# Mamba dt projection: contraction over 16 rows, or over 128 rows with zeros

## Chip, cores, metric

The kernel runs on one core of a Trainium2 chip. The metric is the device time in microseconds of one execution, median of the runs shown.

## What is computed

The program is a stack of layers on an input of shape (2, 256, 56, 56): local attention with convolution, a position term, a six-layer Mamba block with a norm, a gated feed-forward, a causal attention and a mixture of eight experts. Only the Mamba block is touched. Per layer, with 512 inner channels, 16 states and a dt rank of 16:

```python
xz = x @ in_w
u, z = jnp.split(xz, 2, axis=-1)
uc = silu(depthwise_conv4(u) + cb)
x_dbl = uc @ xp_w                      # 48 columns: 16 dt, 16 B, 16 C
dt_r, Bm, Cm = x_dbl[..., :16], x_dbl[..., 16:32], x_dbl[..., 32:]
dt = softplus(dt_r @ dt_w + dt_b)      # the dt projection: contraction over 16
A = -exp(A_log)
h = exp(dt * A) * h + (dt * u) * B     # scan over time, per channel and state
y = sum over states of h * C, plus u * D
out = (y * silu(z)) @ out_w
```

All of it is in float32.

## The kernel before

Three phases follow each other: `conv_phase`, `mamba_phase`, `tail_phase`. They share nothing but tensors in DRAM. In `mamba_phase` the 3136 tokens of an image are cut into 7 chunks of 448 (`T`). The list `chunks` (L788) runs over 2 images, 6 layers and 7 chunks: 84 chunks. Channels lie on the partitions, in 4 blocks (`NB`) of 128.

A chunk has two parts that run one chunk apart. The scan of chunk j takes 32 steps (`order`, L784): each makes its decays on ACT (`decays`, L806), its inputs dt·u·B on POOL (`inputs`, L823, after a small copy of the state by ACT, L822), a scan on DVE (`scan`, L844), the product with C on DVE or, for the 14 steps in `on_pool`, on POOL (L836), a copy of the state on ACT (`keep`, L832). Every second step, `gather` sums over the states on TensorE into the PSUM tile `acc` (L857: four 32-column matmuls beside each other for each pair of tiles); every eighth step it begins with the skip matmul (L852, weights `w_sk`), and `gate` on DVE (L867) multiplies the sum with z. A tile `x` is written by POOL, scanned, multiplied and read by the gather, and only then free again: the pool `mb_x` holds 9.

Between the steps of chunk j lies the preparation of chunk j + 1, each in small pieces: projections of u and z (`project`, L560), convolution by four matmuls with diagonal weights (`u_convolve`, L578), the projection on 48 columns (`x_project`, L610), then the pieces around the change:

- `x_keep` (L618): ACT copies the 48 rows from PSUM into the SBUF tile `xd`; a DMA stores its rows 16 to 47 (B and C) to DRAM (L620), and four more bring them back into `bc`, repeated over partitions (L623).
- `dt_project` (L631), once for each block of 128 channels, in the order 0, 2, 3, 1: one matmul with weights `w_dt` (16 rows by 128 columns) and the first 16 rows of `xd` as moving operand (448 columns).
- `dt_keep` (L637): ACT adds the bias and moves the result from PSUM to SBUF.
- `dt_softplus` (L642) on ACT, `dt_out` (L648 to L652): dt goes to DRAM, POOL forms dt·u (L650), and that goes to DRAM too; `repeat` (L780) brings both back.

All these projections share one PSUM tile, `mm` (pool `mb_pmm`, one buffer), so the next projection waits until ACT has moved the last one out. The order of the instructions on every engine is written by hand: the table `places` gives each piece a place in units of scan steps, `steps` does so for the steps, and all events are sorted by place (L999) and issued in that order. `dt_project` of blocks 0, 2 and 3 lie at 19.3, 20.0 and 20.3, that of block 1 at 22.8; a skip matmul and a gather lie between them.

Weights are loaded once per layer and image by `load_layer` (L510), all DMAs on the queue of SP: `vec`, `w_in`, `w_xp`, `w_dt`, `w_out`, in that order. `w_dt` has one buffer in the pool `mb_weights`, `xd` one in `mb_one`. In the profile a float32 matmul of the program shows as two records (672 records for 336 dt projections).

Of the kernel before, what the change touches and what calls it, by code (L numbers as in the profile page):

```python
# [10 lines left out]
F32 = mybir.dt.float32  # L11
# [7 lines left out]
P = 128  # L19
# [14 lines left out]
DI = 512  # L34
NB = DI // P
DS = 16
DTR = 16
# [15 lines left out]
def chunk(c, n=NT):  # L53
    return slice(c * n, (c + 1) * n)
# [399 lines left out]
def mamba_phase(ctx: ExitStack, tc: tile.TileContext, I, t1_d, t2_d):  # L454
# [8 lines left out]
    nc = tc.nc  # L463
    ctx.enter_context(tc.manual_schedule())
    T, R = MT, MT + 3
    cp = ctx.enter_context(tc.tile_pool(name="mb_const", bufs=1))
    wtp = ctx.enter_context(tc.tile_pool(name="mb_weights", bufs=1))
    one = ctx.enter_context(tc.tile_pool(name="mb_one", bufs=1))
# [36 lines left out]
    def mm():  # L505
        if early[0]:
            return pda.tile([P, 1024], F32, name="da")[:, :512]
        return pmm.tile([P, 512], F32, name="mm", tag="mm")

    def load_layer(layer):  # L510

        vec = wtp.tile([P, V_L], F32, name="vec", bufs=2)
        nc.sync.dma_start(vec, I["mamba_vec"][layer])
        w_in = wtp.tile([P, 2, 2 * DI], F32, name="w_in")
        nc.sync.dma_start(w_in, I["in_w"][layer].rearrange("(k p) o -> p k o", p=P))
        w_xp = wtp.tile([P, NB, DTR + 2 * DS], F32, name="w_xp")
        nc.sync.dma_start(w_xp, I["xp_w"][layer].rearrange("(k p) o -> p k o", p=P))
        w_dt = wtp.tile([DTR, DI], F32, name="w_dt")
        nc.sync.dma_start(w_dt, I["dt_w"][layer])
        w_out = wtp.tile([P, NB, C], F32, name="w_out", bufs=2)  # L520
        nc.sync.dma_start(w_out, I["out_w"][layer].rearrange("(k p) o -> p k o", p=P))
        am = wtp.tile([P, NB * DS], F32, name="am", bufs=2)
        state = wtp.tile([P, NB, 4, 4], F32, name="state", bufs=2)
        tail = wtp.tile([P, NB, 3], F32, name="tail", bufs=2)
        w_sk = wtp.tile([P, NB, P], F32, name="w_sk", bufs=2)
        w_cv = wtp.tile([P, NB * 4, P], F32, name="w_cv")
        L = dict(
            nw=vec[:, 0:2], cb=vec[:, 18:22], dtb=vec[:, 22:26], w_sk=w_sk, w_in=w_in,
            w_xp=w_xp, w_dt=w_dt, w_out=w_out, w_cv=w_cv, am=am, state=state, tail=tail,
        )  # L530
        yield L

        nc.scalar.activation(am, vec[:, 26:90], AF.Exp)
        nc.gpsimd.tensor_scalar(am, am, TINY, -1.0, ALU.max, ALU.mult)
        nc.gpsimd.memset(state, 0.0)
        nc.gpsimd.memset(tail, 0.0)

        for n in range(NB * 4):
            nc.scalar.activation(w_cv[:, n, :], ident, AF.Copy, scale=vec[:, 2 + n : 3 + n])
            if n % 2:  # L540
                yield
        for n in range(NB):
            nc.scalar.activation(w_sk[:, n, :], ident, AF.Copy, scale=vec[:, 90 + n : 91 + n])
            if n % 2:
                yield
# [2 lines left out]

    M = {"dt": cp.tile([P, NB, T + 4], F32, name="dt")[:, :, 3 : T + 3]}
    us = [cp.tile([P, T + 3], F32, name=f"u{n}") for n in range(2)]
    hzs = [cp.tile([P, 2 * NB, T], F32, name=f"hz{n}") for n in range(2)]
# [2 lines left out]
    def project(j, at):  # L556
        Q = QS[j + 1]
        ps = M["mm"] = mm()[:, :T]
        for k in range(2):
# [8 lines left out]
    def u_keep(j, d):  # L568
        tail = layer_of(j + 1)["tail"][:, d, :]
        u = M["u", d] = us[d % 2]  # L570
        nc.scalar.copy(u[:, 0:3], tail)
        nc.scalar.copy(u[:, 3:], M["mm"])
        nc.scalar.copy(tail, u[:, T:])

    def u_convolve(j, d):
        ps = M["mm"] = mm()[:, :T]
        for k in range(4):
            nc.tensor.matmul(  # L578
                ps, lhsT=layer_of(j + 1)["w_cv"][:, 4 * d + k, :], rhs=M["u", d][:, k : k + T],
                start=(k == 0), stop=(k == 3),  # L580
            )

    def hz(j):

        Q = QS[j + 1]
        Q["hz"] = hzs[(j + 1) % 2]
        return Q["hz"]

    def u_add(j, d):
        nc.scalar.activation(  # L590
            hz(j)[:, d, :], M["mm"], AF.Identity, bias=layer_of(j + 1)["cb"][:, d : d + 1]
        )
# [21 lines left out]

    def x_keep(j):

        xd = M["xd"] = one.tile([DTR + 2 * DS, T], F32, name="xd")
        nc.scalar.copy(xd, M["mm"])  # L618
        bc_d = dp.tile([2 * DS, T], F32, name="bc_d")
        nc.sync.dma_start(bc_d, xd[DTR:, :])  # L620
        bc = QS[j + 1]["bc"] = bcs[(j + 1) % 2]
        for n in range(4):
            nc.sync.dma_start(  # L623
                bc[chunk(n, HD), :, :T],
                bc_d.rearrange("(m n) t -> n m t", n=4)[n].unsqueeze(0).to_broadcast([HD, 8, T]),
            )
        QS[j + 1]["dt_d"], QS[j + 1]["dtu_d"] = {}, {}

    def dt_project(j, d):
        ps = M["mm"] = mm()[:, :T]  # L630
        nc.tensor.matmul(  # L631
            ps, lhsT=layer_of(j + 1)["w_dt"][:, chunk(d, P)], rhs=M["xd"][:DTR, :],
            start=True, stop=True,
        )

# [155 lines left out]
    def layer_of(j):  # L791
        return layers[chunks[j][:2]]
# [87 lines left out]
    def load(j):  # L880

        QS[j + 2] = {}
        b, layer, c = chunks[j + 2]
        if (b, layer) not in layers:
            loading[j] = load_layer(layer)
            layers[b, layer] = next(loading[j])
# [5 lines left out]
    def load_rest(j):  # L892
# [12 lines left out]
        (u_project, 3): 12.31697, (u_keep, 3): 12.96717, (u_convolve, 3): 14.04980,  # L905
        (u_add, 3): 14.56347, (z_project, 1): 15.43302, (z_keep, 1): 16.33985, (u_silu,): 17.02689,
        (x_project,): 18.08430, (x_keep,): 18.92340, (dt_project, 0): 19.34668,
        (dt_keep, 0): 19.40825, (dt_project, 2): 20.04090, (dt_keep, 2): 20.17101,
        (dt_project, 3): 20.28119, (dt_keep, 3): 20.60584, (dt_project, 1): 22.80017,
        (dt_keep, 1): 23.31716, (dt_softplus,): 23.33757, (dt_out, 0): 24.14324,  # L910
        (z_project, 2): 24.29994, (z_keep, 2): 24.73754, (z_project, 3): 24.99253,
# [74 lines left out]
    for j in range(nj):  # L986
        b, layer, c = chunks[j]
# [550 lines left out]
```

## Time and profile before

| | us |
|---|---|
| median of 3 runs | 9790.64 (9786.32 to 9806.52) |
| profiled execution, its own time | 9795.2 |
| its span, first to last instruction | 9793.4 |
| Mamba part, from about 614 us to about 8490 us | 7880 |

| engine | busy us | share of the span |
|---|---|---|
| PE (TensorE) | 8175.8 | 83% |
| DVE (VectorE) | 8083.2 | 83% |
| POOL (GpSimd) | 7545.9 | 77% |
| ACT (ScalarE) | 6611.1 | 68% |

In the profile a group of instructions is a line of the kernel, an engine, an operation and its tiles, then the count, the total busy time, the mean of one in ns, and the idle time of the engine ahead of it with what ended it. PEclk is the share of TensorE's clock that its throttle granted, 0.873 over the span. The last part, after 8490 us, is another phase and is bound by TensorE at full clock.

### The profile page before, as it was taken

To read this page: it belongs to the slowest core of one execution; us is meant where nothing else is said; L and a number is where in the kernel's file an instruction comes from. 1 tells how busy PE (TensorE), PEld (TensorE's weight loads), DVE (VectorE), ACT (ScalarE), POOL (GpSimd) and SP (SyncE) were. 2 spreads that over 40 slices of the span, in tenths; PEclk is the share of its full clock that TensorE was granted. 3 is DMA by queue.
4 is the path that set the end of the run, shared out by engine and by line. 5 is a ranking of instruction groups with operands and counts; after the bars stand their busy time and mean duration, and the time that the engine had idled before them with its cause. 6 is when DMAs were issued, how large, how long until landed. Compare 5 with 4: busy or idle time off the path is not lost. (4 is left out here: it accounts for less than half of the span.)

```text
span 9793.4 us, 102137 instructions
## 1 busy us (share of the span) xinstructions
PE 8175.8 (83%) x31362; PEld 3469.1 (35%) x31362; DVE 8083.2 (83%) x6388; ACT 6611.1 (68%) x15130; POOL 7545.9 (77%) x5146
## 2 busy tenths in 40 slices
PE   9878888888888887888888878888888888699999
PEld 6543333332222222333322223222222233255555
DVE  3339999999999999998999999999999999685453
ACT  1127777777777777777777777777777777534443
POOL 1339999899999999999999999999999999511110
PEclk9988888888888888888888888888888888799999
DMA  2235555555555555555555555555555555301111
GB/s 81 68 97 121 119 133 124 135 124 118 132 121 121 130 122 125 127 133 134 131 118 128 126 129 122 124 131 118 132 121 121 133 121 123 107 19 36 42 39 38
DMA packets 681949, 1083.42 MB, mean 111 GB/s; under 512 B 83532, under 2 KB 673169, under 8 KB 681169
## 3 DMA queue, kind: packets, MB, share of 16 engines
q1 hardware_dynamic: 681398, 1076.90, 47.7%
q8 instruction: 246, 4.03, 0.2%
q14 instruction: 305, 2.50, 0.1%
HBM read 891.71 MB, written 184.91 MB: 110 GB/s over the span
## 5 line engine op out<-in xcount | busy, mean ns | idle before, releaser
L823 POOL TENSOR_TENSOR x<-dtur,bc 128x900 f32<-128x900 f32 x2688 | 4712.4, 1781 | 285.4 <-PE acc L857 272.0
L806 ACT ACTIVATE da<-dtr,am 128x451 f32<-128x451 f32 x5376 | 3400.6, 638 | 367.0 <-DVE x L844 220.5
L844 DVE TENSOR_TENSOR_SCAN da<-da,x 128x902 f32<-128x902 f32 x1512 | 3050.7, 2030 | 358.5 <-POOL x L823 176.5
L844 DVE TENSOR_TENSOR_SCAN x<-da,x 128x902 f32<-128x902 f32 x1176 | 2353.9, 2022 | 51.8 <-ACT da L806 34.7
L836 POOL TENSOR_TENSOR x<-x,bc 128x896 f32<-128x896 f32 x1176 | 2074.0, 1773 | 63.0 <-DVE x L844 59.1
L560 PE MATMUL mm<-xn,w_in 128*128 128x448 f32 x2652 | 1344.7, 635 | 494.8 <-ACT hz L590 244.9
L836 DVE TENSOR_TENSOR x<-da,bc 128x896 f32<-128x896 f32 x1512 | 1610.3, 1083 | 83.8 <-ACT state L832 49.4
L857 PE MATMUL acc<-x,sum_w 128*32 128x448 f32 x10752 | 1498.2, 633 | 21.2 <-POOL x L836 18.9
L578 PE MATMUL mm<-u,w_cv 128*128 128x448 f32 x2656 | 1186.0, 593 | 203.3 <-ACT res L715 184.5
L560 PEld LDWEIGHTS mm<-xn,w_in 128*128 128x128 f32 x2652 | 504.3, 211 | 1382.5 <-issue 459.0
L578 PEld LDWEIGHTS mm<-u,w_cv 128*128 128x128 f32 x2656 | 515.8, 204 | 866.4 <-issue 426.2
L631 PE MATMUL mm<-xd,w_dt 16*128 16x448 f32 x664 | 482.8, 817 | 232.8 <-ACT dt L637 134.6
L822 ACT COPY x<-state 128x2 f32<-128x2 f32 x2688 | 466.4, 189 | 287.2 <-PE acc L857 280.5
L857 PEld LDWEIGHTS acc<-x,sum_w 128*32 128x32 f32 x10752 | 268.3, 118 | 1043.4 <-issue 511.7
L708 PE MATMUL mm<-hz,w_out 128*128 128x448 f32 x1344 | 550.4, 552 | 79.6 <-ACT res L715 65.2
L852 PE MATMUL acc<-hz,w_sk 128*128 128x448 f32 x672 | 469.4, 791 | 41.9 <-DVE hz L867 41.8
L832 ACT COPY state<-da 128x2 f32<-128x2 f32 x1512 | 229.5, 157 | 390.0 <-DVE x L836 323.8
L1386 DVE TENSOR_TENSOR hid<-hid,cb 128x784 f32<-128x784 f32 x128 | 140.7, 1101 | 423.3 <-ACT hid L1383 394.5
L610 PE MATMUL mm<-hz,w_xp 128*48 128x448 f32 x664 | 339.6, 666 | 140.0 <-ACT state L832 140.0
L650 POOL TENSOR_TENSOR dtu<-dt,hz 128x448 f32<-128x448 f32 x336 | 325.3, 979 | 125.9 <-ACT state L832 110.6
L590 ACT ACTIVATE hz<-mm,vec 128x448 f32<-128x448 f32 x332 | 207.0, 624 | 277.8 <-PE mm L578 277.8
L708 PEld LDWEIGHTS mm<-hz,w_out 128*128 128x128 f32 x1344 | 241.8, 190 | 395.5 <-issue 189.6
(222 smaller groups left out, 9167.3 us busy)
## 6 DMA issues: line engine op xcount, KB each, us to landing
dtr<-dt_d SPq DMA_DIRECT2D x1344, 224.0 KB
dtur<-dtu_d SPq DMA_DIRECT2D x1344, 224.0 KB
bc<-bc_d SPq DMA_DIRECT2D x336, 448.0 KB
dt_d<-dt SPq DMA_DIRECT2D x336, 224.0 KB
dtu_d<-dtu SPq DMA_DIRECT2D x336, 224.0 KB
cb<-comb_d SPq DMA_DIRECT2D x128, 196.0 KB
t<-t_d SPq DMA_DIRECT2D x28, 448.0 KB
w_in<-in_in_w SPq DMA_DIRECT2D x12, 1024.0 KB
```

The lines of the kernel that those rows point to most:

```text
L560: nc.tensor.matmul(ps, lhsT=layer_of(j + 1)["w_in"][:, k, chunk(at, P)], rhs=Q["xn"][:, k, :], start=(k == 0), stop=(k == 1),)
L578: nc.tensor.matmul(ps, lhsT=layer_of(j + 1)["w_cv"][:, 4 * d + k, :], rhs=M["u", d][:, k : k + T], start=(k == 0), stop=(k == 3),)
L610: nc.tensor.matmul(ps, lhsT=layer_of(j + 1)["w_xp"][:, d, :], rhs=hz(j)[:, d, :], start=(d == 0), stop=(d == NB - 1),)
L631: nc.tensor.matmul(ps, lhsT=layer_of(j + 1)["w_dt"][:, chunk(d, P)], rhs=M["xd"][:DTR, :], start=True, stop=True,)
L708: nc.tensor.matmul(ps, lhsT=layer_of(j - 1)["w_out"][:, d, chunk(k, P)], rhs=QS[j - 1]["hz"][:, d, :], start=(d == 0), stop=False,)
L806: nc.scalar.activation(D[i][:, chunk(g, R)], dtr[:, 2 * pr + g, :], AF.Exp, scale=L["am"][:, col : col + 1],)
L822: nc.scalar.copy(x[:, :, 0:1], states(i))
L823: nc.gpsimd.tensor_tensor(x[:, :, 1:], Q[k][1][:, 2 * pr : 2 * pr + 2, :], wide(Q["bc"][:, ng, :]), ALU.mult)
L836: engine.tensor_tensor(both(X[i])[:, :, 1 : T + 1], both(h)[:, :, 1 : T + 1], wide(QS[j]["bc"][:, 4 + ng, :T]), ALU.mult,)
L844: nc.vector.tensor_tensor_scan(h, D[i], X[i], 0.0, ALU.mult, ALU.add)
L852: nc.tensor.matmul(acc[0][:, :T], lhsT=L["w_sk"][:, k, :], rhs=Q["hz"][:, k, :], start=True, stop=False,)
L857: nc.tensor.matmul(acc[0][chunk(g, HD), :T], lhsT=sum_w, rhs=both(X[i - 1 + g // 2])[:, g % 2, 1 : T + 1], start=False, stop=(ng == 3), ti ...
```

## The change

`xd` and `w_dt` become tiles of 128 rows that are allocated once, in the pool of constants, and set to zero once, by two memsets on POOL at the start of the phase. The copy from PSUM and the load of the weights fill the same rows as before; rows 16 to 127 of `w_dt` stay zero, and so do rows 48 to 127 of `xd`. Rows 16 to 47 of `xd` hold B and C, which the zero rows of `w_dt` multiply. The dt projection contracts over all 128 rows.

```diff
-        w_dt = wtp.tile([DTR, DI], F32, name="w_dt")
-        nc.sync.dma_start(w_dt, I["dt_w"][layer])
+        nc.sync.dma_start(w_dt[:DTR, :], I["dt_w"][layer])
...
-            w_xp=w_xp, w_dt=w_dt, w_out=w_out, w_cv=w_cv, am=am, state=state, tail=tail,
+            w_xp=w_xp, w_out=w_out, w_cv=w_cv, am=am, state=state, tail=tail,
...
+    xd = cp.tile([P, T], F32, name="xd")
+    nc.gpsimd.memset(xd, 0.0)
+    w_dt = cp.tile([P, DI], F32, name="w_dt")
+    nc.gpsimd.memset(w_dt, 0.0)
...
-        xd = M["xd"] = one.tile([DTR + 2 * DS, T], F32, name="xd")
-        nc.scalar.copy(xd, M["mm"])
+        nc.scalar.copy(xd[: DTR + 2 * DS, :], M["mm"])
         bc_d = dp.tile([2 * DS, T], F32, name="bc_d")
-        nc.sync.dma_start(bc_d, xd[DTR:, :])
+        nc.sync.dma_start(bc_d, xd[DTR : DTR + 2 * DS, :])
...
-            ps, lhsT=layer_of(j + 1)["w_dt"][:, chunk(d, P)], rhs=M["xd"][:DTR, :],
+            ps, lhsT=w_dt[:, chunk(d, P)], rhs=xd,
```

## Prediction

> **What bounds the kernel now.** I read the page first, then a long stretch of the Mamba part by engine, the table of waits, the timeline of two chunks, and last the granted clock in short windows.
>
> ```profile
> PEclk9988888888888888888888888888888888799999
> ...
> L631 PE MATMUL mm<-xd,w_dt 16*128 16x448 f32 x664 | 482.8, 817 | 232.8 <-ACT dt L637 134.6
> ```
>
> The matmul to be changed takes 817 ns on average, but its shortest record is 534 ns, and that of w_in (L560: 128 rows, also 448 columns) is 538 ns. So 16 rows cost no less than 128 at one clock, and most of these matmuls run at a lower clock. PEclk is 8 tenths all through the Mamba part.
>
> ```profile
> 2000.00:4000.00 2000.00, 1620.26 (x5723) 593.08 (x5722) 1859.26 (x1231) 1562.12 (x3705) 1860.01 (x1127) 0.86 0.56 125
> ```
>
> ```profile
> POOL x L823 <- PE acc L857: 272.0, 112, 5.2
> DVE da L844 <- POOL x L823: 176.5, 70, 3.1
> ```
>
> The first fence is 2 ms of the Mamba part: busy us of PE, PEld, DVE, ACT and POOL, then the clock. DVE and POOL are both 93% busy and set the pace; a chunk (from one copy of xd to the next) takes 92.4 us on average, 85 us of it work of each. What can be won is the other 7 us. The second fence, from the table of waits, says that POOL waits for TensorE's accumulation (L857), and DVE for POOL in turn. By offset in the chunk (my count over 81 chunks, from the trace) POOL's wait sits nearly all in one place: 8 to 12 us after the copy of xd, 2.56 us a chunk; DVE idles 2.9 us a chunk in the stage from that copy to the softplus. That is the stage of the dt projections. One of each kind:
>
> ```profile
> 4000.47 1.01 PE L631 MATMUL mm<-xd,w_dt 16*128 16x448 f32 x2 [0.61 <-ACT xd L618]
> 4002.39 1.85 PE L631 MATMUL mm<-xd,w_dt 16*128 16x448 f32 x2 [0.90 <-ACT dt L637]
> 4004.97 1.85 PE L631 MATMUL mm<-xd,w_dt 16*128 16x448 f32 x2 [0.72 <-ACT dt L637]
> 4006.75 1.86 PE L852 MATMUL acc<-hz,w_sk 128*128 128x448 f32 x2
> 4008.55 1.72 PE L857 MATMUL acc<-x,sum_w 128*32 128x448 f32 x8
> ```
>
> ```profile
> 2085.68 1.01 PE L631 MATMUL mm<-xd,w_dt 16*128 16x448 f32 x2 [0.61 <-ACT xd L618]
> ...
> 2089.34 1.01 PE L631 MATMUL mm<-xd,w_dt 16*128 16x448 f32 x2 [0.72 <-ACT dt L637]
> 2090.28 1.68 PE L852 MATMUL acc<-hz,w_sk 128*128 128x448 f32 x2
> 2091.89 1.72 PE L857 MATMUL acc<-x,sum_w 128*32 128x448 f32 x8
> ```
>
> In the first chunk the clock halves after the first projection: 1.01 becomes 1.85 us, and skip matmul and gather (L852, L857), in order behind them, take 1.86 and 1.72 us where 0.92 and 0.96 us are seen elsewhere at full clock. The gather ends 9.80 us after the first projection began. The second chunk, one of two with three fast projections, ends it after 7.93 us. POOL's wait falls from 2.91 to 1.07 us, DVE's idle time in the stage from 3.25 to 1.48: 1.8 us each for 1.87 us of gather. These two chunks are also the shortest of all (88.4 us).
>
> **Why the clock falls there.** The clock changes only at steps of 3.41 us. Cut at those steps (PE busy, then the clock granted in that window):
>
> ```profile
> 3906.40:3909.82 3.42, 3.42 (x6) 0.50 0.30 55
> 3909.82:3913.23 3.41, 1.89 (x5) 1.00 0.08 19
> 3913.23:3916.65 3.42, 2.70 (x5) 0.50 1.02 200
> 3957.60:3961.02 3.42, 1.77 (x5) 1.00 0.00 0
> 3961.02:3964.43 3.41, 2.46 (x7) 1.00 0.00 0
> 4005.39:4008.80 3.41, 3.41 (x8) 0.50 1.07 208
> 4008.80:4012.22 3.42, 3.25 (x10) 0.50 0.90 163
> ```
>
> A full window of x_project (128 rows) at half clock is followed by full clock. 1.89 us busy, mostly 16-row matmuls, is followed by half; 1.77 us of 128-row matmuls keeps full. The window at 4005.39 is full, a third of it 16-row work, and the clock stays at half. Counted over the whole Mamba part, with each matmul's streaming time as its share of the window: at full clock and a share of 0.4 to 0.6, 155 windows without 16-row work all kept the clock, and 61 of the 62 with a tenth or more of it lost it. At half clock and a share of 0.85 or more, all 254 without recovered, 9 of 58 with it did. The border between keeping and losing lies at 0.33 to 0.40. Matmuls of few rows hardly count as activity. The start of the kernel says the same:
>
> ```profile
> 19.81 17.40 PE L181 MATMUL mm<-pew,qn 5*112 5x256 f32 x40 [7.94 <-ACT pe L186]
> 41.03 21.45 PE L236 MATMUL mm<-xg,wqkv 128*128 128x448 f32 x50 [1.16 <-ACT rs L221]
> ```
>
> Five rows back to back for 17.4 us stay at 0.43 us for 256 columns; the 128-row matmuls reach 0.376 us for 448 columns within 6 us.
>
> **The change, part by part.** The order of instructions on every engine is unchanged but for two memsets on POOL and one wait.
>
> Matmul with 128 rows, 336 of them (672 records): at one clock 538 against 534 ns, so 672 x 4 ns = 3 us of TensorE time, behind DVE and POOL: 0. The Trainium skill says the same (TensorE: Matmul & The Clock Gate, "Why this matters for your kernels": K=32 takes the time of K=128), and its Part 1 lets the clock depend on how busy TensorE was, with no word of rows. By that rule the change is worth nothing: 9790 us. The windows above speak against it, and I follow them.
>
> What the clock then does. If padded rows count, the windows that lost the clock in this stage (80 at full clock that reach into its first three projections; 78 lost it) are judged by their whole share: 62 of the 80 are above 0.385. The next window then holds two projections (0.44) or projection, skip and gather (more). I take 70% of chunks as fast throughout, the rest as losing the clock midway; there skip and gather with the fourth projection behind them are dense enough to win it back, since the fourth counts too.
> Fast throughout, the gather ends at 2090.28 - 2085.68 + 0.92 + 0.96 - 0.07 (overlap) = 6.4 us after the first projection, 1.5 us earlier than the better chunk, and POOL's 1.07 us there go. So 70% of chunks wait 0 and 30% about 1.2 us as the better chunk does: 0.4 us on average instead of 2.56. DVE falls from 2.9 to about 0.5. The smaller gain counts, as both are needed: 2.2 us x 84 chunks = 185 us.
>
> What is late next: the multiplication of dt by u on POOL (L650) waits 1.3 us a chunk for ACT and stays. Half clock at x_project, the norm and the y projections belongs to other sparse windows and stays; only its place shifts.
>
> The memsets (448 and 512 columns): POOL's 128x128 memset took 0.20 us and 128x16 0.11, so 0.8 ns a column and 0.5 us each. POOL is idle from 614.57 to 627.96, so they are hidden; without that cover, 1 us once. The first load of w_dt (617.43 on SP) now also waits for them; they end near 615.6, so it waits 0. If it waited, the loads of w_out and the next t behind it would wait as long, at most some us once. Copy into xd, the DMA of B and C and the reloads of w_dt keep their forms and their single buffers: 0.
>
> The sum, for the profiled execution: 9795.2 - 185 = 9610; its median stands 4.6 us lower: 9605.
>
> **Rivals.** (1) Rows of zeros don't count. For it: nothing in the trace is zero in both operands. Against: in the spread matmuls (L682, 112 rows) the moving operand is an identity, 1 of 112 non-zero, and in 13 windows at half clock the share reaches 0.83 only with them; all recovered. The diagonal w_cv weights, 127 of 128 zero, keep the clock like dense ones. The skill tells of data dependence only for its peak-current limit (Part 1: all-zero operands don't trip it), another throttle than this one by its states; if this gate were of that kind, 9790. (2) The window after the first often loses the clock all the same, as ACT paces the projections about 1.9 us apart (0.746 us streaming in 1.92: 0.39, on the border). Then half of the delay stays or moves elsewhere: 0.5 to 1.1 us x 84 = 40 to 90 us, 9700 to 9750. (3) Slower: chunks lock to the clock's steps. 18 of 81 chunks last 95.2 to 95.8 us, in runs; 28 steps are 95.57 us, so each meets the same slow windows as the last. If shorter stages led all chunks into that lock, 3.2 us x 84 = 269 us more: about 10060. It takes over half of the chunks in the lock to eat the 185 us. Against: such chunks hold 2 to 4 us of idle time in this very stage, and without it they would not close at 28 steps.
>
> **Numbers.** Rows count and it works: 0.80, 9470 to 9700 (lower end: the shortest chunks' 88.4 us everywhere, (92.4 - 88.4) x 84 = 336 us, 9455; upper end: half the gain). Rival 2: 0.06. Rival 1: 0.08. Rival 3: 0.06. Faster by over 0.2%, which is about what a measurement can tell here: 0.86. The range reaches from 9450 into rival 2, to 9770.
>
> **What would show it.** Granted clock in the Mamba part up from 0.86 to about 0.90; mean of the dt matmul down from 817 to 560 to 650 ns; POOL's wait for L857 down from 272 to some 90 us; DVE and POOL above 95% busy. Clock unchanged would show rival 1; clock up with the same chunk length, a wait that I have not seen.

## The result, and the profile after

| | before | after |
|---|---|---|
| median | 9797.51 us (4 runs, 9786.32 to 9806.52) | 9678.35 us (4 runs, 9673.57 to 9687.3) |
| ratio after to before | | 0.988 (95% interval 0.9863 to 0.9897) |
| profiled execution, own time / span | 9795.2 / 9793.4 us | 9687.3 / 9685.5 us |
| TensorE's mean clock over the span | 0.873 | 0.896 |

The medians are now those of the runs measured side by side. The change makes the kernel 1.2% faster: 119 us by the medians, 108 us by the two profiled spans. The forecast was 9605, with 9450 to 9770 as its range; about two thirds of the expected gain came.

First the row of granted clock and the group of the changed matmul, from the page of the changed kernel (line numbers are 2 higher than before):

```profile
PEclk9978888888888888888888889889888888799999
...
L633 PE MATMUL mm<-xd,w_dt 128*128 128x448 f32 x664 | 386.6, 668 | 260.1 <-ACT dt L639 134.5
```

The mean of one dt matmul fell from 817 to 668 ns although it now reads eight times as many rows. Where the clock is full it costs as much as before, which the timeline of TensorE shows: start, duration, instruction, then its idle time before. The first six rows are a chunk that loses the clock after its first projection, the next five a chunk that keeps it. The last two belong to a third chunk, which keeps it as well and differs in the row ahead of its first projection, `x_project` (L613); the filler ahead of `x_project` comes back to it.

```profile
4027.95 3.21 PE L613 MATMUL mm<-hz,w_xp 128*48 128x448 f32 x8 [1.98 <-ACT state L834]
4032.85 1.02 PE L633 MATMUL mm<-xd,w_dt 128*128 128x448 f32 x2 [1.69 <-ACT xd L620]
4034.76 1.84 PE L633 MATMUL mm<-xd,w_dt 128*128 128x448 f32 x2 [0.89 <-ACT dt L639]
4037.33 1.86 PE L633 MATMUL mm<-xd,w_dt 128*128 128x448 f32 x2 [0.72 <-ACT dt L639]
4038.98 1.70 PE L854 MATMUL acc<-hz,w_sk 128*128 128x448 f32 x2
4040.61 1.44 PE L859 MATMUL acc<-x,sum_w 128*32 128x448 f32 x8
...
4126.88 1.02 PE L633 MATMUL mm<-xd,w_dt 128*128 128x448 f32 x2 [1.68 <-ACT xd L620]
4128.79 1.02 PE L633 MATMUL mm<-xd,w_dt 128*128 128x448 f32 x2 [0.89 <-ACT dt L639]
4130.54 1.02 PE L633 MATMUL mm<-xd,w_dt 128*128 128x448 f32 x2 [0.72 <-ACT dt L639]
4131.39 0.92 PE L854 MATMUL acc<-hz,w_sk 128*128 128x448 f32 x2
4132.24 0.96 PE L859 MATMUL acc<-x,sum_w 128*32 128x448 f32 x8
...
2139.07 4.90 PE L613 MATMUL mm<-hz,w_xp 128*48 128x448 f32 x8 [1.98 <-ACT state L834]
2144.59 1.02 PE L633 MATMUL mm<-xd,w_dt 128*128 128x448 f32 x2 [0.61 <-ACT xd L620]
```

A projection takes 1.02 us at full clock, against 1.01 with 16 rows, and 1.84 to 1.86 at half. In the second chunk the gather ends 4132.24 + 0.96 - 4126.88 = 6.32 us after the first projection began; in the first one 9.20 us, as in the first chunk shown of before (9.80). The next view cuts TensorE's time at the steps of 3.41 us (busy time, count, granted clock); its first row is the long stretch of the Mamba part with all engines (PE, PEld, DVE, ACT, POOL, then the clock).

```profile
2000.00:4000.00 2000.00, 1597.23 (x5781) 597.56 (x5781) 1884.65 (x1248) 1579.86 (x3761) 1888.62 (x1146) 0.88 0.57 126
...
4031.40:4034.82 3.42, 1.08 (x3) 1.00 0.07 17
4034.82:4038.23 3.41, 2.69 (x3) 0.50 0.84 177
4038.23:4041.64 3.41, 3.41 (x12) 0.50 1.08 203
4041.64:4045.06 3.42, 1.36 (x6) 1.00 0.88 160
...
4126.97:4130.39 3.42, 1.95 (x4) 1.00 0.30 81
```

The window at 4126.97 is busy for 1.95 us, nearly all of it dt projections, and the clock stays; before, 1.89 us of them lost it (the window at 3909.82 in the prediction). The window at 4031.40 begins in the gap behind `x_project`, holds little more than one projection, 1.08 us, and the clock falls. The full window at 4038.23 brings it back, too late for the gather. DVE and POOL are 94.2% and 94.4% busy in the 2 ms, against 93.0% before. And from the table of waits (waiting instruction, what released it, total us, how often, longest us):

```profile
POOL x L825 <- PE acc L859: 135.0, 66, 5.0
POOL dtu L652 <- ACT state L834: 113.8, 83, 2.4
```

POOL's wait for the gather is half of its 272.0 us; its wait ahead of dt·u (110.6 us before) is as it was.

The stage in both kernels, as means over 81 chunks of the trace (my count, same method as in the prediction; "three fast" are chunks whose first three projections all ran at full clock; gather end is from the start of the first projection; the clock is counted from the first copy of xd to the last):

| | chunk us | gather end us | POOL idle in stage us | DVE idle in stage us | clock in the Mamba part | three fast |
|---|---|---|---|---|---|---|
| before | 92.37 | 9.34 | 2.56 | 2.90 | 0.853 | 2 |
| after | 91.01 | 7.40 | 1.21 | 1.32 | 0.883 | 48 |
| its 48 chunks with three fast | 90.87 | 6.32 | 0.45 | 0.80 | | |
| its other 33 | 91.22 | 8.97 | 2.32 | 2.08 | | |

1.36 us less a chunk, times 84 chunks, is 114 us, which covers the difference of the spans (108 us) and of the medians (119 us). So the gain comes from this stage, most of it at least: DVE idles 1.58 us less in it, and 0.26 us more in the rest of the chunk (4.32 before, 4.58 after).

The two groups of the changed kernel's own chunks do not show what one kept stage is worth. The 48 are 0.35 us shorter than the 33, though DVE idles 1.28 us less in their stage; single chunks scatter by about 2.5 us, and DVE idles more after the stage in the 48 (4.80 against 4.24 us). The worth of the stage is read between kernels here, not between chunks.

### The profile page after: what moved, and what is told of

Its sections match the earlier page's. It is cut to its first block, busy times and chain, and to the rows that moved or that the text cites. A ratio compares the mean times of both kernels' runs of the same rounds, so it can differ in the third digit from the quotient of the medians.

```text
span 9685.5 us, 102140 instructions
## 1 busy us (share of the span) xinstructions
PE 7986.8 (82%) x31362; PEld 3436.8 (35%) x31362; DVE 8079.1 (83%) x6388; ACT 6603.3 (68%) x15130; POOL 7545.5 (78%) x5148
## 5 line engine op out<-in xcount | busy, mean ns | idle before, releaser
L859 PE MATMUL acc<-x,sum_w 128*32 128x448 f32 x10752 | 1478.3, 625 | 21.4 <-POOL x L838 19.0
L633 PE MATMUL mm<-xd,w_dt 128*128 128x448 f32 x664 | 386.6, 668 | 260.1 <-ACT dt L639 134.5
L854 PE MATMUL acc<-hz,w_sk 128*128 128x448 f32 x672 | 420.1, 715 | 44.9 <-DVE hz L869 44.6
L613 PE MATMUL mm<-hz,w_xp 128*48 128x448 f32 x664 | 318.8, 631 | 132.8 <-ACT state L834 132.8
L652 POOL TENSOR_TENSOR dtu<-dt,hz 128x448 f32<-128x448 f32 x336 | 325.1, 978 | 127.0 <-ACT state L834 113.8
```

What stands on the lines that cost most here:

```text
L633: nc.tensor.matmul(ps, lhsT=w_dt[:, chunk(d, P)], rhs=xd, start=True, stop=True,)
L854: nc.tensor.matmul(acc[0][:, :T], lhsT=L["w_sk"][:, k, :], rhs=Q["hz"][:, k, :], start=True, stop=False,)
L859: nc.tensor.matmul(acc[0][chunk(g, HD), :T], lhsT=sum_w, rhs=both(X[i - 1 + g // 2])[:, g % 2, 1 : T + 1], start=False, stop=(ng == 3), ti ...
```

## Experiments

Theory: the clock that TensorE is granted follows its matmuls weighed by their active rows, whatever the values in them; the 16-row projections counted for next to nothing, the padded ones count in full, and the clock acts on the time through the gather that POOL waits for. Rivals: the values count, so that part of the effect comes only with real numbers; there is a threshold of rows instead of a weight; the gain has nothing to do with the clock but with a cost of changing between shapes of matmul. And for the missing third of the gain: other half-clock windows of the chunk, the order of the instructions, or the fourth projection. All edits are to the changed kernel unless said otherwise. The counts of chunks come from the trace of each kernel's one profiled execution; where the interval is not given in the text it is in the table at the end of this section.

**How many rows, and what is in them.** Three kernels contract over part of the padded rows (32 here; 64 and 96 likewise):

```diff
-            ps, lhsT=w_dt[:, chunk(d, P)], rhs=xd,
+            ps, lhsT=w_dt[:32, chunk(d, P)], rhs=xd[:32, :],
```

> The dt projection contracts over 32 rows of the padded tiles instead of 128. Theory P (TensorE's activity counts in proportion to the rows in use): a quarter of the share, so windows of dt projections still fall below 0.33; granted clock in the Mamba part 0.85 to 0.86, mean of the dt matmul about 800 ns, time as before (9780 to 9805). Theory S (a step: any matmul with more than 16 rows, or more than a certain number, counts in full): 9680, clock 0.88, if the step lies at 32 or below, else as before.

> 64 rows. Theory P: half of the share, 0.22 instead of 0.44 for two projections in a window: the clock is still lost in nearly all chunks; a part of the slow windows (full ones with skip and gather) recovers one step earlier, so 9730 to 9790. Theory S with a step at 64 or below: 9680, as with 128 rows.

> 96 rows. Theory P: three quarters of the share, 0.33 for two projections, at the border; windows with a piece of x_project keep the clock, others lose it; 9700 to 9770, between the kernel before and the changed one. Theory S with a step at 96 or below: 9680. A theory without the clock [...]: 9680 here too, with the clock where it was.

A fourth fills the rows with numbers that are not zero. It changes the computation: rows 16 to 127 add 112 more products to each dt projection.

```diff
-    nc.gpsimd.memset(xd, 0.0)
+    nc.sync.dma_start(xd[DTR + 2 * DS :, :], I["x"][0, : P - DTR - 2 * DS].rearrange("c h w -> c (h w)")[:, :T])
...
-    nc.gpsimd.memset(w_dt, 0.0)
+    nc.sync.dma_start(w_dt[DTR:, :], I["in_w"][0][: P - DTR, :DI])
```

> 128 rows, but the padding is not zero: rows 48 to 127 of xd hold values of the input x and rows 16 to 127 of w_dt values of in_w, loaded once, so the projection has 112 more products in its sum (its values differ from the reference's). Theory Z0 (zeros count like data): same time as the changed kernel, 9665 to 9695, clock in the Mamba part 0.88. Theory Z1 (zeros count less): more windows keep the clock, clock 0.89 or more, 9600 to 9660.

The group of the dt matmul on the pages of the kernels with 32 rows and with 96 rows:

```profile
L633 PE MATMUL mm<-xd,w_dt 32*128 32x448 f32 x664 | 478.7, 811 | 233.8 <-ACT dt L639 134.4
```

```profile
L633 PE MATMUL mm<-xd,w_dt 96*128 96x448 f32 x664 | 429.2, 735 | 256.1 <-ACT dt L639 134.4
```

The mean of one goes 817, 811, 788 (64 rows), 735, 668 (128 rows of zeros), 657 ns (128 rows of numbers): it falls with the rows, by far most of it in the last two steps. The times: 9786.5 us with 32 rows, 0.9993 (0.9984 to 1.0001), no gain that can be told; 9763.25 with 64, 0.9968 (0.9956 to 0.9979), a little; 9696.0 with 96, 0.990 (0.9885 to 0.9914), most of it, a little below the 9700 to 9770 forecast for a weight in proportion; 9668.82 with 128 rows of numbers, 0.9876 (0.9861 to 0.989).

The windows of 3.41 us say it more directly. As in the prediction, the share of a window is the streaming time in it over 3.41 us, and only windows with a tenth or more of dt work are taken:

| rows | full clock, share 0.4 to 0.6: kept the clock | half clock, share 0.85 or more: recovered |
|---|---|---|
| 16 | 1 of 62 | 9 of 58 |
| 32 | 3 of 58 | 12 of 59 |
| 64 | 5 of 61 | 12 of 50 |
| 96 | 61 of 87 | 56 of 63 |
| 128, zeros | 68 of 68 | 24 of 24 |
| 128, numbers | 72 of 73 | 21 of 21 |

If a dt matmul is given a weight and the borders are held at those that the other windows show (lost below 0.37, regained above 0.80), the weight that sorts most windows rightly is 0.0 for 16 rows, 0.1 for 32, anything from 0.2 to 0.45 for 64, 0.75 for 96, 1.05 and 0.95 for the two with 128. The values in the middle are loose: other borders, and other ways to place the streaming time in the windows, give 0 to 0.25 for 16 rows, 0.05 to 0.7 for 32, 0.5 to 0.85 for 64 and 0.7 to 0.9 for 96. So it is shown that the weight rises with the rows, from near nothing at 16 to full at 128; that it rises in proportion is compatible with the counts and not shown. One threshold of rows does not fit: 64 rows gain a little, and 96 keep most windows, yet not all as 128 do. Real data add nothing to zeros (0.9876 and 0.988, intervals one on the other). A cost of changing between shapes of matmul is not needed: with three projections at full clock the gather ends at 6.32 us, where 6.4 had been worked out from durations of the kernel before; and with 96 rows the clock in the Mamba part rose to 0.880, where that theory left it as it was.

With 96 rows only 12 chunks have three fast projections and POOL idles 1.53 us in the stage, 0.32 more than with 128 rows, which times 84 is 27 us; the median is 18 us higher, with intervals that touch. That its chunk is no longer than that of the change (90.93 and 91.01 us) says little: the profiled execution with 96 rows was the fastest of its four (9680.87 us), that of the change the slowest of its four (9687.3).

**The other windows at half clock.** Four kernels put extra matmuls, whose results nobody reads, into windows where TensorE is sparse: after the first three dt projections (two of 64 columns each), ahead of the norm's inverse, ahead of `x_project`, and all three together.

```diff
-        ps = M["mm"] = mm()[:, :T]
+        bank = mm()
+        ps = M["mm"] = bank[:, :T]
...
+        if d != 1:
+            for n in range(2):
+                nc.tensor.matmul(
+                    bank[:, T:], lhsT=ident, rhs=mean_w[:, : 512 - T], start=True, stop=True
+                )
```

> The changed kernel, and after the dt projections of blocks 0, 2 and 3 two more matmuls each of 128 rows and 64 columns of constants, into the 64 columns of the PSUM bank that nobody reads; TensorE waits about 0.9 us there for ACT anyway. Only the share of busy windows rises (0.44 to about 0.55 for two projections). If the 33 of 81 chunks that still lose the clock are what is missing from the forecast: chunks with all projections fast from 48 to 70 or more, DVE's idle time in the stage from 1.3 to 0.8 us, 9620 to 9650. If what the stage wins is lost again elsewhere in the chunk: clock up, 9665 to 9690.

```diff
+    fill = cp.tile([P, T], F32, name="fill")
+    nc.gpsimd.memset(fill, 1.0)
...
+        if key == "n":
+            nc.tensor.matmul(
+                M["mm"][:, 512 - T :], lhsT=mean_w, rhs=fill, start=True, stop=True
+            )
```

> The changed kernel, and one more matmul of 128 rows and 448 columns of constants (into columns of the norm's PSUM bank that nobody reads) in each norm of the next chunk, where TensorE waits for POOL's power; the one-column matmuls there leave a window at a share of 0.2 and the clock falls. If slow windows anywhere cost DVE and POOL time: clock in the Mamba part 0.90 or more, 9620 to 9660. If only the dt stage's are on the path: clock up, 9665 to 9690.

```diff
-        ps = M["mm"] = mm()[: DTR + 2 * DS, :T]
+        bank = mm()
+        ps = M["mm"] = bank[: DTR + 2 * DS, :T]
+        for n in range(2):
+            nc.tensor.matmul(bank[:, :T], lhsT=mean_w, rhs=fill, start=True, stop=True)
```

> The changed kernel, and two more matmuls of 128 rows and 448 columns of constants ahead of x_project, into the bank that x_project then overwrites, where TensorE waits about 2 us for ACT's silu. If slow windows anywhere cost time: x_project at full clock ends 1.5 us earlier in most chunks, DVE's idle time ahead of the copy of xd falls from 1.6 to about 1 us; 9610 to 9650. If not on the path: 9665 to 9690.

> All three fillings together. If each is worth what its stage waits: clock 0.95 or more in the Mamba part, chunk about 89 us, 9500 to 9570. If only the clock rises: 9650 to 9690.

The filler in the dt stage gave 59 chunks with three fast projections instead of 48 and 9660.83 us, 0.9864 (0.985 to 0.9879): 17 us below the change, with intervals that overlap, and between the two times forecast for it. It cannot give much, since in its good chunks the gather ends at 7.38 us instead of 6.32: the fillers stand in the way of what they speed up.

The filler at the norm raised the clock and not the speed. The same 2 ms of it, all engines:

```profile
2000.00:4000.00 2000.00, 1590.73 (x5840) 592.51 (x5840) 1887.54 (x1250) 1582.80 (x3765) 1893.46 (x1149) 0.90 0.56 126
```

The clock over the stretch is 0.90 (0.897 over the Mamba part, from 0.883), DVE and POOL do nearly the same work in it as in the changed kernel, and the time is 9670.12 us, 0.9876 (0.986 to 0.9893). All fillers together reach 0.905 and take 9723.19 us, more than no filler and above both times forecast for them. So a higher clock as such is worth nothing here. Of the stages tried it counts in that of the dt projections, where POOL waits for the gather.

The filler ahead of `x_project` made it worse: 9725.73 us, 0.993 (0.9915 to 0.9945), 47 us above the change, with 22 chunks of three fast projections. Neither theory had expected that. The timeline of TensorE in one of its chunks:

```profile
4145.79 3.21 PE L618 MATMUL mm<-hz,w_xp 128*48 128x448 f32 x8 [0.29 <-ACT state L839]
4150.68 1.02 PE L638 MATMUL mm<-xd,w_dt 128*128 128x448 f32 x2 [1.68 <-ACT xd L625]
4152.59 1.71 PE L638 MATMUL mm<-xd,w_dt 128*128 128x448 f32 x2 [0.89 <-ACT dt L644]
```

`x_project` now runs at full clock in all 81 chunks (3.21 us; 4.90 at half), as wished. But the first projection does not follow it sooner by as much, since it waits for ACT's copy of `xd`, and that has its place behind decays in ACT's order. ACT in the chunk of the change whose `x_project` ends at 4031.16:

```profile
4031.02 1.31 ACT L808 ACTIVATE da<-dtr,am 128x451 f32<-128x451 f32 x2
4032.27 0.52 ACT L620 COPY xd<-mm 48x448 f32<-48x448 f32 x1
```

So TensorE stands empty for 1.68 us ahead of the first projection, where 0.61 us are seen after an `x_project` at half clock (2144.59 above), and a window that holds this gap and one projection loses the clock. The counts bear it out. In the change, all 27 chunks with `x_project` at half clock have three fast projections, of those where the clock changes within it 5 of 8, and of those with `x_project` at full clock 16 of 46. In the five other kernels with 128 rows that have chunks with `x_project` at half clock, all 150 of these have three fast projections. Here no chunk is of that kind, and 22 of 81 keep the clock. In 53 of the other 59 the window that lost it began ahead of the first projection and was streaming for at most 0.33 of its length.

**The order of the instructions.** If only the gather carries the clock's effect to POOL, then the gather can be freed of it with no padding at all: the third projection is issued behind skip matmul and gather, and its copy out of PSUM later on ACT. The edit was made in the kernel before and in the changed one:

```diff
-        (dt_project, 3): 20.28119, (dt_keep, 3): 20.60584, (dt_project, 1): 22.80017,
+        (dt_project, 3): 20.40000, (dt_keep, 3): 21.40000, (dt_project, 1): 22.80017,
```

> The kernel before (16 rows), with the dt projection of block 3 issued behind the skip matmul and the gather instead of ahead of them (and its move by ACT two small copies later). The clock is left as it is. Theory G (what costs time is that the gather stands in TensorE's queue behind three projections, so that POOL gets its tiles late): the gather ends about 2 us earlier at half clock, POOL's wait in the stage falls from 2.6 to below 1 us a chunk, 9620 to 9690 with the granted clock still about 0.85 in the Mamba part. Theory K (the clock itself is the limit, by other ways than the gather): 9770 to 9800.

> The same move in the changed kernel. Theory G: the gather ends below 5 us after the first projection in fast chunks and about 7 in slow ones, the remaining wait of POOL in the stage (1.2 us a chunk) falls to about 0.3; up to 0.9 us x 84 = 75 us less than the changed kernel, 9600 to 9650. Rival: the padding has already taken what the gather can give, and the late fourth projection delays the softplus: 9660 to 9720.

In the kernel before, 9754.68 us, 0.9963 (0.9949 to 0.9977), which lies between the two forecasts: a gain of 38 us, though the gather ends 2.65 us earlier (6.69 instead of 9.34). Two waits of the kernel before stand first, then the table of waits of the moved one (its profiled execution took 9781.35 us, the longest of its five):

```profile
POOL dtu L650 <- ACT state L832: 110.6, 83, 3.4
DVE da L844 <- issue: 16.2, 8, 3.3
```

```profile
POOL dtu L650 <- ACT state L832: 257.1, 83, 5.9
DVE da L844 <- issue: 128.3, 62, 2.5
POOL x L823 <- PE acc L857: 84.3, 65, 4.6
```

POOL's wait for the gather is down from 272.0 to 84.3 us at an unchanged clock (0.849). So that wait was of the gather. But the wait ahead of dt·u grew from 110.6 to 257.1 us, and DVE's scan waits 128.3 us where it waited 16.2. The timelines of TensorE, ACT and DVE in one chunk show how:

```profile
4094.83 1.86 PE L631 MATMUL mm<-xd,w_dt 16*128 16x448 f32 x2
...
4096.72 0.63 ACT L637 ACTIVATE dt<-mm,vec 128x448 f32<-128x448 f32 x1 [1.54 <-PE mm L631]
4097.26 2.54 ACT L806 ACTIVATE da<-dtr,am 128x451 f32<-128x451 f32 x4
...
4099.88 2.04 DVE L844 TENSOR_TENSOR_SCAN da<-da,x 128x902 f32<-128x902 f32 x1 [2.26 <-issue]
```

ACT stands 1.54 us at `dt_keep`, which waits for a projection at half clock; four decays queue behind it on ACT and end at 4099.80; DVE's scan begins at 4099.88. The profile names no releaser for that wait; the scan reads the decays' tile. So the slow projections reach the time by two ways: through the gather to POOL, and through `dt_keep` on ACT to the decays and to dt·u. Taking the first away exposes the second. That the clock is in this second way too, and not only the new order, is seen with the same order in the changed kernel.

In the changed kernel the same move gives 9615.68 us, 0.9819 (0.9805 to 0.9834), within the forecast of theory G (9600 to 9650) and the best of all kernels here: 63 us below the change and 177 us below the kernel before. Its waits and its timeline of TensorE:

```profile
POOL dtu L652 <- ACT state L834: 131.4, 83, 2.7
DVE da L846 <- issue: 44.4, 61, 0.7
POOL x L825 <- PE acc L859: 52.4, 26, 4.6
```

```profile
4095.37 1.02 PE L633 MATMUL mm<-xd,w_dt 128*128 128x448 f32 x2 [1.68 <-ACT xd L620]
4097.28 1.02 PE L633 MATMUL mm<-xd,w_dt 128*128 128x448 f32 x2 [0.90 <-ACT dt L639]
4098.98 0.96 PE L859 MATMUL acc<-x,sum_w 128*32 128x448 f32 x8
4099.87 1.02 PE L633 MATMUL mm<-xd,w_dt 128*128 128x448 f32 x2
```

The gather ends 4.57 us after the first projection here (4.75 on average), the first three projections stay at full clock in 72 of 81 chunks, and with the same order as in the kernel before the wait ahead of dt·u is 131.4 us instead of 257.1, that of DVE's scan 44.4 instead of 128.3. Two counts go with the 72: no chunk loses the clock behind its first projection any more (5 did in the change), now that skip and gather follow the second at once, and only 27 chunks instead of 46 have `x_project` at full clock; why they became fewer was not looked into. The two edits are worth 38 and about 119 us alone and 177 together, some 20 us more than their sum, which is little against the intervals.

**The fourth projection.** The prediction let the fourth projection help to win the clock back. Here it keeps its 16 rows:

```diff
-            ps, lhsT=w_dt[:, chunk(d, P)], rhs=xd,
+            ps, lhsT=w_dt[: (DTR if d == 1 else P), chunk(d, P)], rhs=xd[: (DTR if d == 1 else P), :],
```

> A part of the change alone: 128 rows in the projections of blocks 0, 2 and 3, 16 rows in that of block 1, behind the gather. If the fourth matters only where a lost clock has to be won back: the share of chunks that stay fast is as in the changed kernel, the others stay slow for a window more; 9680 to 9710. If it carries a good part of the gain: 9720 or more.

9686.66 us, 0.9891 (0.9876 to 0.9906), with 42 chunks of three fast projections: as forecast for the case that the fourth matters only where a lost clock has to be won back, and not to be told from the change.

**All in one table** (medians; the kernel before was run beside each group; the last four columns from the trace of one execution, which took 9680.87 us for 96 rows, 9697.75 with all fillers and 9781.35 for the move with 16 rows, some way from those medians):

| kernel | us | ratio to before | chunk us | DVE idle in stage us | clock | three fast |
|---|---|---|---|---|---|---|
| 32 rows | 9786.5 | 0.9993 (0.9984 to 1.0001) | 92.32 | 2.83 | 0.853 | 7 |
| 64 rows | 9763.25 | 0.9968 (0.9956 to 0.9979) | 92.12 | 2.66 | 0.859 | 9 |
| 96 rows | 9696.0 | 0.990 (0.9885 to 0.9914) | 90.93 | 1.82 | 0.880 | 12 |
| 128 rows, numbers | 9668.82 | 0.9876 (0.9861 to 0.989) | 90.98 | 1.27 | 0.882 | 52 |
| filler, dt | 9660.83 | 0.9864 (0.985 to 0.9879) | 90.75 | 1.57 | 0.891 | 59 |
| filler, norm | 9670.12 | 0.9876 (0.986 to 0.9893) | 90.92 | 1.35 | 0.897 | 47 |
| filler, x_project | 9725.73 | 0.993 (0.9915 to 0.9945) | 91.48 | 1.87 | 0.883 | 22 |
| all fillers | 9723.19 | 0.9923 (0.9907 to 0.994) | 91.23 | 1.96 | 0.905 | 46 |
| moved, 16 rows | 9754.68 | 0.9963 (0.9949 to 0.9977) | 92.18 | 2.23 | 0.849 | 6 |
| moved, padded | 9615.68 | 0.9819 (0.9805 to 0.9834) | 90.13 | 0.76 | 0.887 | 72 |
| fourth with 16 rows | 9686.66 | 0.9891 (0.9876 to 0.9906) | 91.05 | 1.43 | 0.881 | 42 |

By and large, the rows with 96 rows and with the dt filler apart, the time follows the idle time of the stage, and not the clock: of the two kernels with the most clock, 0.905 is slower than the change and 0.897 not to be told from it, and the fastest has 0.887.

## Why the prediction was right, and where it was not

- **What a padded matmul costs.** Forecast: as much as one of 16 rows at one clock. A projection takes 1.02 us against 1.01. Right.
- **Rows count for the clock, and zeros count.** Right, and shown by the count of windows (68 of 68 kept, before 1 of 62), by the row of kernels with 32 to 128 rows and by the kernel with numbers in the rows. Rival 1 falls. The Trainium skill's rule (TensorE: Matmul & The Clock Gate, Part 1), that the gate goes by how busy TensorE was, with no word of rows, would have given no change; the measured windows decide against it for matmuls of few rows.
- **The gather in a chunk that keeps the clock.** Forecast 6.4 us after the first projection, measured 6.32. Right.
- **Share of chunks that keep it.** Forecast 70%, measured 48 of 81, 59%. Too high. The count behind it, 62 of 80 windows above 0.385, used windows of the kernel before, in which `x_project` ran at full clock in 31 of 81 chunks. The forecast let the half clock at `x_project` stay. It did not: 46 chunks have `x_project` at full clock now, and those are the ones with a gap of about 1.6 us ahead of the first projection; 30 of the 33 chunks that lose the clock are among them, and none has `x_project` at half clock. Why `x_project` meets the full clock more often was not tested.
- **What is left in the rest.** Forecast: these chunks lose the clock midway, skip and gather win it back, POOL waits 1.2 us. Measured: the gather ends at 8.97 us on average (5 of the 33 at 8.0, as forecast, 28 between 8.8 and 9.2), and POOL waits 2.26 us for it. This is the step that failed most. The 28 lose the clock in a window that begins 1.1 to 2.2 us ahead of the first projection and was streaming for 0.22 to 0.33 of its length, as the one at 4031.40; two projections, the skip matmul and most of the gather then run at half clock. That is not rival 2, whose window begins with the projections and lies at 0.39: by that one the other 5 lose it (0.37 to 0.40). The forecast had such windows in its count (18 of its 80 lie below 0.385), but let every slow chunk lose the clock midway, as its better chunk does, and gave the gap ahead of the first projection no term.
- **No wait in the good chunks.** Forecast 0. POOL waits 0.15 us for the gather there. The rest of the 0.45 us that it idles in the stage is nearly all the beginning of its next wait, ahead of dt·u.
- **The sum.** Forecast for POOL's wait: 0.3 x 1.2 = 0.36 us on average, so 2.2 us saved a chunk. Measured: 0.41 x 2.26 + 0.59 x 0.15 = 1.01 us, so 1.55 us saved in the stage, of which 1.36 come out as a shorter chunk. Of the 0.84 us between 2.2 and 1.36, the longer wait of the slow chunks is 0.41 x (2.26 - 1.2) = 0.43, the share 0.11 x 1.2 = 0.13, the wait of the good ones 0.59 x 0.15 = 0.09, and 0.19 us is won in the stage and not by the chunk. Times 84 chunks that is 71 us, most of the 73 us between 9605 and 9678. This is bookkeeping of waits; it does not show that saving the 33 chunks would bring their share in full, and the filler that saved 11 of them brought 17 us, within the noise. The mechanism was right and the size of the term was off.
- **The memsets.** Forecast 0.5 us each, hidden. Measured 0.47 and 0.53 us, the second ending at 617.54 instead of 615.6 (the phase begins 2.1 us later in this execution); the load of w_dt is issued at 619.59, after that of w_xp in SP's order. Right: 0.
- **What stays.** POOL's wait ahead of dt·u: 110.6 and 113.8 us. Right. But I had taken it as ACT's own lateness; the moved kernels show that part of ACT's lateness can be the clock too.
- **The signs to look for.** Clock in the Mamba part about 0.90: it came to 0.883. Dt matmul 560 to 650 ns: 668. POOL's wait for the gather some 90 us: 135. DVE and POOL above 95%: 94.2 and 94.4. All in the forecast's direction and short of it, as would follow from the chunks that still lose the clock.
- **Rival 3, chunks locking to the steps at 95.6 us.** Not seen: no chunk lasts 95.2 to 95.8 us any more. But chunks do fall in with the steps at a shorter length: 20 of 81 last 88.6 to 88.9 us (26 steps are 88.75 us), none did before.

## What to carry to other kernels

Where TensorE is sparse and something in order waits for it, count what its clock sees: matmuls that contract over few rows run as long as full ones and hardly hold the clock, and rows of zeros, which cost nothing at one clock, made them count. A higher clock by itself was worth nothing here; read which instruction waits for TensorE in the stage, and ask by which second way (here ACT's copy out of PSUM and what queues behind it) the same slow matmuls reach the time. With a clock that is judged in steps of 3.41 us, look also at the gap ahead of the sparse stage: when the start of the stage is fixed by another engine's order (here ACT's copy of `xd`), matmuls that end sooner can do no more than widen that gap, and here the window around it lost the clock in most cases.

## What was not expected of the hardware

- The weight of a matmul for the clock grows with its rows: windows with dt projections kept the full clock in 1 of 62 with 16 rows, 5 of 61 with 64, 61 of 87 with 96 and 68 of 68 with 128. Whether the rows hold zeros or numbers made no difference (68 of 68 and 72 of 73).
- More TensorE work ahead of a sparse stage can leave that stage with less clock, since `x_project` at full clock widens the gap ahead of it from 0.61 to about 1.6 us: with fillers ahead of `x_project`, chunks with three fast projections fell from 48 to 22 and the time rose by 47 us.
- Taking away a wait of 188 us in all (272.0 to 84.3) gave 38 us; 147 us came back as POOL's wait ahead of dt·u and 112 us as DVE's wait for its scan.
